# Fifteen products of the identity by itself on TensorE in the opening of a macaron block

## The chip, the cores and the metric

The kernel runs on one core of one Trainium2 chip. The metric is device time in microseconds (us) of one execution of the whole program; lower is better. The time before is the median of three runs. The profile is of one further execution.

## What is computed

The reference is a block of three residual steps over x, 2048 tokens of 1024 values in float32: half a feed-forward step, an attention step over a three-tap convolution, and the same feed-forward step again. The change touches the opening of the first feed-forward step, so that part is what must be seen:

```python
def _L0_ffn_ref(x, weight, bias, gate_w, in_channel_scale, out_channel_scale):
    ...
    router_logits = xf @ gate_w.T
    routing = jax.nn.softmax(router_logits.astype(jnp.float32), axis=1).astype(x.dtype)
    in_scale = routing @ in_channel_scale
    out_scale = routing @ out_channel_scale
    wb = ste_sign(weight)
    out = xf * in_scale @ wb.T * out_scale + bias
...
x = x + 0.5 * _L0_ffn_ref(_layernorm(x, axis=-1), L0_ffn_weight, ...)
x = x + _L0_attn_ref(_layernorm(x, axis=-1), ...)
x = x + 0.5 * _L0_ffn_ref(_layernorm(x, axis=-1), L0_ffn_weight, ...)
```

There are 8 experts, so the router's logits are 8 columns wide. The main product takes the sign of a 1024 x 1024 weight.

## The kernel before

The tokens are worked in 16 tiles of 128 rows. Each tile of a feed-forward step goes through the same stages, which are methods of the class `Ffn`:

- `norm_sums` takes mean and variance on VectorE (`bn_stats`, L164), the power on GpSimd (L171), and hands back a function that applies the normalization (on VectorE, L177, for the first tiles). The result is the tile `xn_f`.
- `transpose` (L216) turns `xn_f` on TensorE by products with the identity in transpose mode, eight of 128 x 128, four to a PSUM bank `tr_f`. ScalarE copies each bank to `xnT_f` (L217).
- `gate` (L224) multiplies by the gate's weights: eight products into four groups of 32 columns of `lgp_f`. ScalarE copies the result to `lgs` (L232).
- `route` (L237 to L249) adds the four groups by one product with `fold` (`lg_f`), takes the maximum on VectorE (L239), the exponential on ScalarE (`ro_f`, L242), and splits the routing into two parts (`rhl_f`).
- `turn` (L256) transposes the routing on TensorE (`rt_f`); VectorE copies it to `rT_f` (L258).
- `scale` (L268) makes the input scale of each channel by eight products `is_f` of `rT_f` with `tables`; VectorE multiplies (L279), ScalarE casts (`y_f`, L281), and the remainder is taken on VectorE or GpSimd (L282).
- `main` (L307) is the big product: for each of eight chunks, two halves of 512 columns and two parts of `y_f`, against `sw`, the signs of the weight. VectorE scales the sums and adds them to x (L319, L320).

The signs are made by ScalarE from the loaded weight rows (`sign`, L653, 1024 columns at a time). `tables` comes from two small tensors, worked on ScalarE (L136) and VectorE (L140, L146).

The opening is in the function `begin` (from L640). It is written in an order of its own: inside `tc.manual_schedule()` (L746) every instruction is issued on its engine in the order of the program text. `begin` issues the loads: the gate's rows on ScalarE's queue (L659), x and the weight on SyncE's queue (L660 to L669), the tables on GpSimd's queue (L130). Then it transposes the gate's rows (`gt`, L674, eight products with an output of 128 x 8 each), copies them to `gate_sb` (L675), and takes tiles 0 and 1 step by step through the stages up to the big product of tile 0 (L719), in which the stages of tiles 1 and 2 are placed between chunks (`beside`, L711). Behind `begin`, `ffn.run(2)` works the remaining tiles.

`ident` is the 128 x 128 identity in float32 that GpSimd makes at the very start (L106). PSUM tiles come from four pools of two banks each, "mm", "acc", "tr" and "sm", through the function `bank` (L73); a pool gives out its two buffers in turn. In the opening, "acc" is first used by `out_scale` (`po_f`, L291).

Of the kernel before, what the change touches and what calls it, by code (L numbers as in the profile page):

```python
# [17 lines left out]
P = 128  # L18
# [6 lines left out]
def kernel(  # L25
# [22 lines left out]
    nc = tc.nc  # L48
# [24 lines left out]
    def bank(kind, shape, name):  # L73
        return banks[kind].tile(shape, F32, name=name, tag=kind)
# [21 lines left out]
    def load_x(t):  # L96
        x1[t] = xring.tile([P, D], F32, name=f"x1_{t}", tag="x1")
        nc.sync.dma_start(out=x1[t], in_=x[ts(t, P), :])
# [6 lines left out]
    ident = const.tile([P, P], F32, name="ident")  # L105
# [12 lines left out]
    def small_constants():  # L118
        nc.vector.tensor_copy(fold, ident[:, 0:E])
        for j in range(1, 4):  # L120
            nc.vector.tensor_tensor(fold, fold, ident[:, ds(j * QC, E)], ALU.add)
        half = ident.rearrange("p (g h j) -> p g h j", g=4, h=2)[:, :, 1, :]
        nc.vector.tensor_reduce(lower, half, AX.XY, ALU.add)
        nc.vector.tensor_scalar(sides, lower, -2.0, 1.0, ALU.mult, ALU.add)

    def table_loads(raw):

        for n, src in enumerate((ics, ocs)):
            for h in range(NH2):
                nc.gpsimd.dma_start(  # L130
                    out=raw[ts(2 * n + h, QC), :],
                    in_=src[:, ts(h, NB)].unsqueeze(0).broadcast_to([4, E, NB]),
                )

    def upper_terms(raw, upper, n):
        nc.scalar.copy(upper[ts(n, P // 2), :], raw[ts(n, P // 2), :])  # L136

    def lower_terms(raw, n):
        at = ts(n, P // 2)
        nc.vector.tensor_scalar(raw[at, :], raw[at, :], lower[at, :], None, ALU.mult)  # L140

    def table_terms(raw, upper, n):


        at = ts(n, P // 2)
        nc.vector.scalar_tensor_tensor(  # L146
            tables[at, :], upper[at, :].bitcast(F32), sides[at, :], raw[at, :], ALU.mult, ALU.add
        )
# [35 lines left out]
    class Ffn:  # L184
# [13 lines left out]
        def norm(self, t, pinned=False, on_vector=False):  # L198
            for n in range(t, min(t + 2, self.end)):
                self.ahead(n)  # L200
            self.norm_sums(t, pinned, on_vector)()
# [207 lines left out]
    def x2_sums(t):  # L409
        xn = x2ns[t] = xnp.tile([P, D], F32, name=f"x2n_{t}", tag="xn")  # L410
        x2[t] = spill.tile([P, D], F32, name=f"x2_{t}")
        nc.sync.dma_start(out=x2[t], in_=x1[t])

        return sums_of(xn, x1.pop(t), f"x2_{t}", on_vector=2 * (t + 1 == NT))
# [225 lines left out]
    def begin(ffn, work):  # L640

        raws = {}

        def load_raw(c):
            pl, tag = (cwp, "cw") if c < 6 else (xring, "x1")
            raws[c] = pl.tile([P, D], F32, name=f"raw_{c}", tag=tag)
            nc.sync.dma_start(out=raws[c], in_=weight_t[ts(c, P), :])

        def sign(*chunks):
            for c in chunks:
                nc.scalar.activation(sw[:, c, :], raws[c], AF.Sign)  # L653


        rows = work.tile([P, D], F32, name="gate_rows", tag="osc")[0:DC, :]
        tmp = work.tile([P, D], F32, name="tables_raw", tag="osc")
        raw, upper = tmp[:, 0:NB], tmp[:, NB:D].bitcast(F32R)
        nc.scalar.dma_start(out=rows, in_=gate_t.rearrange("(c p) e -> c (p e)", p=P))  # L659
        load_x(0)  # L660
        load_x(1)
        for c in range(DC):
            load_raw(c)
            if c == 5:
                load_x(2)
        nc.sync.dma_start(out=hbias, in_=bias.broadcast_to([P, D]))
        load_x(3)
        load_x(4)
        load_x(5)  # L669
        table_loads(raw)  # L670
        small_constants()
        gt = bank("sm", [P, E, DC], "gt")
        for e in range(E):
            nc.tensor.transpose(gt[:, e, :], rows.rearrange("c (p e) -> c e p", e=E)[:, e, :], ident[0:DC, 0:DC])  # L674
        nc.scalar.copy(gate_sb[:, :, 0:E], gt.rearrange("p e c -> p c e"))  # L675
        on_vector = (nc.vector.tensor_copy,) * 2
        ffn.norm_sums(0, on_vector=2)()
        norm = ffn.norm_sums(1, on_vector=1)
        ffn.transpose(0)
        norm()  # L680
        ffn.gate(0)
        upper_terms(raw, upper, 0)
        ffn.route(0, lambda: lower_terms(raw, 0))
        table_terms(raw, upper, 0)
        ffn.transpose(1)
        ffn.turn(0)
        sign(0, 1)
        ffn.scale(0, lows=(nc.vector, nc.gpsimd))
        upper_terms(raw, upper, 1)
        lower_terms(raw, 1)  # L690
        table_terms(raw, upper, 1)
        ffn.gate(1)
        sign(2)
        norms = {}

        def part(*steps):
            def run():
                for stage, *a in steps:
                    stage(*a)
            return run  # L700

        def halve():
            nc.scalar.mul(hbias, hbias, 0.5)

        def sums(t, on_vector=False):
            norms[t] = ffn.norm_sums(t, on_vector=on_vector)

        def apply(t):
            norms.pop(t)()

        beside = {  # L711
            1: part((sign, 3), (ffn.route, 1), (sums, 2, 1)),
            2: part((sign, 4), (apply, 2)),
            3: part((ffn.turn, 1), (sign, 5)),
            4: part((sign, 6), (ffn.scale, 1), (sign, 7), (halve,), (ffn.add_bias, 1)),
            5: part((ffn.transpose, 2, on_vector), (sums, 3, 1)),
            6: part((ffn.out_scale, 0), (ffn.gate, 2)),
        }
        ffn.main(0, 0, 1, beside=beside, apart=DC - 2)  # L719
        ffn.add_bias(0)  # L720
        apply(3)
        ffn.out_scale(1)
        ffn.add_bias(2)
        rest = []
        ffn.main(1, 0, beside={
            2: part((ffn.route, 2), (sums, 4)),
            4: part((ffn.transpose, 3), (apply, 4), (ffn.add_bias, 4)),
            6: part((ffn.turn, 2)),
        })
        ffn.gate(3)  # L730
        ffn.scale(2, out=True)
        ffn.add_bias(3)
        ffn.main(1, 1, beside={
            3: part((ffn.route, 3), (ffn.transpose, 4)),
            5: part((ffn.turn, 3)),
            6: lambda: (rest.append(x2_sums(0)), sums(5)),
        })
        ffn.gate(4)
        rest[0]()
        apply(5)  # L740
        ffn.add_bias(5)

    with ExitStack() as ph:
        work = pool(ph, "work1", 2, side="right")
        ffn = Ffn("f1", sw, work, xnp, 0, NT, lambda t: x1[t], next_x, norm_x2, transpose_x2, beside)
        with tc.manual_schedule():  # L746
            begin(ffn, work)
        for dst, src in ((conv_b_sb, conv_b), (bq_sb, bq), (bk_sb, bk), (bv_sb, bv), (bo_sb, bo)):
            tc.keep_in_program_order(nc.sync.dma_start(out=dst, in_=src))
        ffn.run(2)  # L750
# [331 lines left out]
```

## Time and profile before

| what | value |
|---|---|
| median of three runs | 976.1 us (974.65 to 977.55) |
| profiled execution, its own time | 974.22 us |
| span of the profiled execution | 972.0 us |
| DMA, first slice of 24.3 us | 337 GB/s |
| DMA over the whole span | 141 GB/s |
| identity ready (end of its last step on GpSimd) | 1.54 us |
| end of the gate's transposes on TensorE | 4.15 us |
| start of the first transposes of tile 0 | 7.41 us |
| start of the first big product of tile 0 | 16.68 us |

The span runs from the first to the last instruction that the profile shows; the time of an execution has a little around it (974.22 against 972.0). Times inside the execution are counted from the span's start. A row of the timeline names the engine, the line of the kernel, the output and the inputs, their shapes, and in brackets how long the engine sat idle before it and who released it. The chain of waits is the sequence of work that ended last, followed back from the last instruction; each step is either an instruction or the gap between two ("issue"). Engines: PE is TensorE (PEld its loads of the stationary operand), DVE is VectorE, ACT is ScalarE, POOL is GpSimd, SP is SyncE.

### The profile page before, as it was taken

Reading aid. Unit: us, or ns where it says so; the run is one execution under the profiler, and the core shown is the slowest. Engines: PE = TensorE matmul, PEld = TensorE weight load, DVE = VectorE, ACT = ScalarE, POOL = GpSimd, SP = SyncE. Lnnn points to the kernel's source line nnn. Section 1 sums busy time; section 2 is a strip of 40 time slices with the busy share of each in tenths; the row PEclk is TensorE's granted clock in tenths of the full one; section 3 lists DMA queues with packets and bytes.
Section 4 is the critical chain, followed back from the end, with each engine's and each line's share of the span. In section 5 each row is a group of like instructions: output and inputs, shape, how many; then the busy total and the mean of one; then the engine's idle time right before and its main releaser. Section 6 shows DMA issues by size and latency. Waiting matters only on the chain.

```text
span 972.0 us, 13861 instructions
## 1 busy us (share of the span) xinstructions
PE 952.3 (98%) x5064; PEld 623.5 (64%) x5064; DVE 638.0 (66%) x1228; ACT 409.6 (42%) x1122; POOL 250.4 (26%) x319
## 2 busy tenths in 40 slices
PE   6999999999999999999999999999999999999997
PEld 4688778876666666645555455545554556878776
DVE  5788887799986566537656455646555655666654
ACT  5586665421111111126545344536451653444441
POOL 2555443410011101004213121212122312444341
PEclk9999999999999999999999999999999999999999
DMA  9776554698487665235020430044004216646331
GB/s 337 173 199 192 154 174 145 240 246 329 153 260 204 176 172 139 77 134 203 27 104 1 169 109 5 1 157 146 1 0 154 56 31 219 171 135 174 104 109 65
DMA packets 37522, 137.21 MB, mean 141 GB/s; under 512 B 4872, under 2 KB 5896, under 8 KB 35536
## 3 DMA queue, kind: packets, MB, share of 16 engines
q1 hardware_dynamic: 28336, 98.69, 27.9%
q0 software_dynamic: 8384, 29.63, 16.1%
q10 hardware_dynamic: 736, 8.02, 2.2%
q8 instruction: 40, 0.66, 0.3%
q14 instruction: 26, 0.21, 0.1%
HBM read 81.70 MB, written 37.85 MB: 123 GB/s over the span
## 4 chain that ended last, share of the span: by engine, by line
PE 60%; issue 27%; POOL 5%; DVE 3%; DMA 2%; ACT 2%; POOLq 0%; DVEq 0%; ACTq 0%
PE pm_f L307 22%; PE cv L540 22%; POOL xr L857 3%; PE tr_f L216 3%; PE pp L991 2%; PE lgp_f L224 2%; DMA x<-in_x_dram 2%; POOL p L913 2%; PE acc L972 2%; PE is_f L268 1%; PE tr L427 1%; PE pq L880 1%; PE ao L955 1%; PE pt L942 1%; DVE st_f L164 1%
## 5 line engine op out<-in xcount | busy, mean ns | idle before, releaser
L307 PE MATMUL pm_f<-sw,y_f 128*128 128x512 f32 x1024 | 261.5, 406 | 0.6 <-ACT y_f L281 0.4
L307 PEld LDWEIGHTS pm_f<-sw,y_f 128*128 128x128 f32 x1024 | 187.1, 190 | 43.9 <-ACT y_f L281 0.8
L540 PE MATMUL cv<-v,u 128*128 128x342 f32 x576 | 166.0, 450 | 0.0
L540 PEld LDWEIGHTS cv<-v,u 128*128 128x128 f32 x576 | 109.0, 189 | 56.9 <-issue 0.3
L913 POOL TENSOR_SCALAR_AFFINE_SELECT p<-p 128x512 f32<-128x512 f32 x64 | 39.8, 646 | 280.9 <-ACT p L911 280.9
L926 ACT ACTIVATE p<-p,anm 128x128 f32<-128x128 f32 x256 | 99.0, 388 | 16.7 <-DVE anm L923 16.7
L282 POOL TENSOR_TENSOR y_f<-xnT_f,y_f 128x512 fp32r<-128x512 f32 x63 | 79.8, 1282 | 64.8 <-ACT y_f L281 64.8
L319 DVE TENSOR_TENSOR pm_f<-pm_f,os_f 128x512 f32<-128x512 f32 x64 | 44.6, 697 | 70.9 <-PE pm_f L307 70.7
L557 ACT ACTIVATE m<-cv 128x342 f32<-128x342 f32 x42 | 19.2, 457 | 158.7 <-PE cv L540 148.5
L911 ACT COPY p<-sc 128x512 f32<-128x512 f32 x64 | 34.3, 588 | 111.5 <-PE sc L901 111.4
L923 DVE TENSOR_REDUCE anm<-p 128x4 f32<-128x512 f32 x64 | 40.9, 681 | 47.6 <-POOL p L913 47.6
L972 PE MATMUL acc<-oT,wo_sb 128*128 128x512 f32 x128 | 67.2, 616 | 0.4 <-DVE oT L964 0.4
L880 PE MATMUL pq<-qkv,wq_sb 128*128 128x512 f32 x128 | 61.0, 596 | 0.0
L880 PE MATMUL pq<-qkv,wk_sb 128*128 128x512 f32 x128 | 60.1, 592 | 0.0
L540 PE MATMUL cv<-v,g 128*128 128x342 f32 (+2 forms) x224 | 57.1, 415 | 0.9 <-DVE v L462 0.9
L991 PE MATMUL pp<-pw_sb,o2T 128*128 128x512 f32 x128 | 57.4, 599 | 0.4
L864 PE MATMUL pv<-wv_sb,qkv 128*128 128x512 f32 x128 | 56.1, 592 | 0.0
L217 ACT COPY xnT_f<-tr_f 128x512 f32<-128x512 f32 x62 | 35.9, 587 | 47.7 <-PE tr_f L216 47.7
L540 PEld LDWEIGHTS cv<-v,g 128*128 128x128 f32 x224 | 39.7, 190 | 17.6 <-DVE v L462 1.3
L528 DVE SCALAR_TENSOR_TENSOR u<-g,u 128x1024 f32<-128x1024 f32 x18 | 22.0, 1220 | 41.5 <-issue 23.5
L926 ACT ACTIVATION_READ_ACCUMULATOR p<-p,anm 128x1 f32 x256 | 47.8, 187 | 0.0
L934 DVE TENSOR_TENSOR p<-p,asum 128x512 f32<-128x512 f32 x64 | 45.6, 712 | 2.2
(138 smaller groups left out, 1462.7 us busy)
## 6 DMA issues: line engine op xcount, KB each, us to landing
g<-in_conv_w_dram SPq DMA_DIRECT2D x28, 512.0 KB, 4.9
u<-in_conv_w_dram POOLq DMA_DIRECT2D x24, 512.0 KB, 6.1
x<-in_x_dram SPq DMA_DIRECT2D x16, 512.0 KB, 4.6
raw<-in_weight_t_dram SPq DMA_DIRECT2D x16, 512.0 KB, 6.0
x<-hbias POOLq DMA_DIRECT2D x16, 512.0 KB, 5.5
x<-x SPq DMA_DIRECT2D x16, 512.0 KB, 4.3
xr<-x SPq DMA_DIRECT2D x16, 512.0 KB, 6.9
x<-xr SPq DMA_DIRECT2D x16, 512.0 KB, 3.2
```

The lines of the kernel that those rows point to most:

```text
L282: lows[h].tensor_tensor(yl, y, yh.bitcast(F32), ALU.subtract)
L307: ins = nc.tensor.matmul(pms[h], lhsT=y[:, n, c, :], rhs=self.sw[:, c, ts(h, NB)], start=(c == 0 and n == 0), stop=(c == DC - 1 and n == 1),)
L319: nc.vector.tensor_tensor(pms[h], pms[h], o, ALU.mult)
L540: nc.tensor.matmul(accs[w, k][:, lo:hi], lhsT=uk[:, c, :], rhs=V[k][:, c, lo:hi], start=(c == 0), stop=(c == DC - 1),)
L864: nc.tensor.matmul(pv, lhsT=qkvs[g][2][:, c, ts(b, P)], rhs=wv_sb[:, c, ts(half, NB)], start=(c == 0), stop=(c == WC - 1),)
L880: nc.tensor.matmul(pq, lhsT=w_sb[:, c, ts(hp, P)], rhs=qkvs[g][n][:, c, :], start=(c == 0), stop=(c == WC - 1),)
L913: nc.gpsimd.affine_select(out=p, in_=p, pattern=[[0, BPG], [-1, P]], compare_op=ALU.is_ge, fill=NEG_INF, base=0, channel_multiplier=1,)
L923: nc.vector.tensor_reduce(nmax, p, AX.X, ALU.max, negate=True)
L926: nc.scalar.activation(p[:, b, :], p[:, b, :], AF.Exp, bias=nmax[:, b : b + 1], accum_out=asum[:, b : b + 1],)
L934: nc.vector.tensor_tensor(p, p, asum.unsqueeze(2).broadcast_to([P, BPG, P]), ALU.mult)
L972: nc.tensor.matmul(accs[g][m], lhsT=wo_sb[:, hp, ts(m, P)], rhs=oT, start=(hp == 0), stop=(hp == NHP - 1),)
L991: nc.tensor.matmul(pp, lhsT=o2T[:, m, ts(b, P)], rhs=pw_sb[:, m, ts(h, NB)], start=(m == 0), stop=(m == WC - 1),)
```

## The change

A PSUM tile `idle` of 128 x 128 is taken from the pool "acc", and a function `keep_busy` multiplies the identity by itself into it, so many times. It is called in seven places of `begin`: three products ahead of the gate's transposes and six behind them, one between gate and routing of tile 0, one ahead of and two behind the turn of tile 0, and two behind the gate of tile 1. Nothing reads the tile `idle`. The order of the other instructions on TensorE, and everything on the other engines, stays as it is. The first of the products waits for GpSimd, which the gate's transposes did before.

```diff
         small_constants()
+        idle = bank("acc", [P, P], "idle")
+
+        def keep_busy(times):
+
+            for _ in range(times):
+                nc.tensor.matmul(idle, lhsT=ident, rhs=ident, start=True, stop=True)
+
+        keep_busy(3)
         gt = bank("sm", [P, E, DC], "gt")
         for e in range(E):
             nc.tensor.transpose(gt[:, e, :], rows.rearrange("c (p e) -> c e p", e=E)[:, e, :], ident[0:DC, 0:DC])
         nc.scalar.copy(gate_sb[:, :, 0:E], gt.rearrange("p e c -> p c e"))
+        keep_busy(6)
         on_vector = (nc.vector.tensor_copy,) * 2
         ffn.norm_sums(0, on_vector=2)()
         norm = ffn.norm_sums(1, on_vector=1)
         ffn.transpose(0)
         norm()
         ffn.gate(0)
+        keep_busy(1)
         upper_terms(raw, upper, 0)
         ffn.route(0, lambda: lower_terms(raw, 0))
         table_terms(raw, upper, 0)
         ffn.transpose(1)
+        keep_busy(1)
         ffn.turn(0)
+        keep_busy(2)
         sign(0, 1)
         ffn.scale(0, lows=(nc.vector, nc.gpsimd))
         upper_terms(raw, upper, 1)
         lower_terms(raw, 1)
         table_terms(raw, upper, 1)
         ffn.gate(1)
+        keep_busy(2)
         sign(2)
```

## The prediction

> **What bounds the kernel now.** I read the page from the top. TensorE is busy 98% of the span, so almost everywhere a microsecond moves the end only if it is TensorE's own. The exception is the opening, the first slice of the page.
>
> ```profile
> span 972.0 us, 13861 instructions
> PE 952.3 (98%) x5064; PEld 623.5 (64%) x5064; DVE 638.0 (66%) x1228; ACT 409.6 (42%) x1122; POOL 250.4 (26%) x319
> ...
> PE   6999999999999999999999999999999999999997
> ...
> PEclk9999999999999999999999999999999999999999
> ```
>
> See the single 6 at the left: TensorE is less than 70% busy in the first 24.3 us. The clock row reads full there; the next view, the TensorE timeline of the opening, says otherwise (start, length, operation, count):
>
> ```profile
> 3.13 1.02 PE L674 MATMUL gt<-ident,gate_rows 8*128 8x8 f32 x8 [3.13 <-DMA gate_rows<-in_gate_t_dram]
> 7.41 1.97 PE L216 MATMUL tr_f<-ident,xn_f 128*128 128x128 f32 x8 [3.26 <-DVE xn_f L177]
> ...
> 11.54 1.95 PE L216 MATMUL tr_f<-ident,xn_f 128*128 128x128 f32 x8
> ...
> 20.04 3.76 PE L307 MATMUL pm_f<-sw,y_f 128*128 128x512 f32 x8
> ...
> 25.98 0.67 PE L268 MATMUL is_f<-rT_f,tables 32*128 32x128 f32 x8 [0.26 <-DVE rT_f L258]
> ...
> 27.64 1.05 PE L216 MATMUL tr_f<-ident,xn_f 128*128 128x128 f32 x8
> ```
>
> The same eight transposes take 1.95 to 1.97 us up to 13.5 us and 1.05 us at 27.64. Taking off the last one's own length (median 0.27 us warm, up to 0.475 us cold), one follows another after 0.216 us early and 0.111 us late. The 512-column products between 20.6 and 25.1 us start 0.426 us apart; later sixteen take 3.83 us, 0.24 each. So TensorE runs at half speed until somewhere between 25.1 and 26.0 us, although the granted-clock row shows 1.00 all along. I read the clock from the spacing, not from that row.
>
> Last, the chain of waits of the opening, which says whose time counts:
>
> ```profile
> 7.41 1.98 PE tr_f L216 x8
> ...
> 10.05 0.69 PE lgp_f L224 x8
> ...
> 11.09 0.59 PE lg_f L237 x2
> 11.69 1.81 PE tr_f L216 x8
> 13.50 0.02 issue
> 13.52 0.59 ACT xnT_f L217
> 14.11 1.90 ACT sw L653 x2
> 16.01 0.00 issue
> 16.02 0.63 ACT y_f L281
> ...
> 25.73 0.21 DVE rT_f L258
> 25.94 0.04 issue
> 25.98 0.67 PE is_f L268 x6
> ```
>
> From 7.41 to 13.50 TensorE has 5.07 us of the chain. From 13.52 to 25.73 it has none: ScalarE and VectorE carry it (signs, casts, router and norm of the next tiles). From 25.98 on TensorE is the chain again. So the slow products from 16.7 to 25.7 cost nothing; only the slow work before 13.5 us can be won.
>
> **The change part by part.** Fifteen products are added on TensorE and nothing else: order and waits of the other four engines stay as they are. Their output takes one buffer of the two-buffer pool "acc", so the users after it swap their two banks; no wait is added, cost nothing.
>
> Price of one: the trace has no 128x128 f32 product with a full stationary operand, but it shows that an f32 product is issued as two matrix instructions (lg_f: one call, x2), and each is a 128-column pass like a transpose. So 2 x 0.216 = 0.43 us slow, 2 x 0.111 = 0.22 us fast. Ends: 0.43, and 0.50 if loads don't overlap (two loads of lg_f: 0.50 us). I take 0.43, the transpose being the nearer shape.
>
> - Three before the gate's transposes. The identity is ready at 1.54 us: 1.6 to 2.9 us, beside the wait for gate_rows (3.13). At 0.50 each they end at 3.1. Hidden; gate_sb is ready at 5.74 and first needed at 9.31.
> - Six behind them: from 4.15 us, 6 x 0.43 = 2.6, to 6.75 (7.15 at 0.50). The transposes of tile 0 wait for xn_f until 7.41. Hidden, with 0.3 to 0.7 us to spare.
> - One after the gate of tile 0: its waiter, lg_f, waits for ScalarE until 11.09; lgp_f ends at 10.74. Hidden.
> - One before and two after the turn (rt_f), two after the gate of tile 1: what they cost depends on the clock, below. The last two stand before products that are not on the chain; free.
>
> What they can win is the clock. **If TensorE is fast from 7.4 us**, I walk the chain again. Transposes of tile 0: the second half of xn_f comes at 7.81, so they end at 7.85 + 3 x 0.111 + 0.27 = 8.46 instead of 9.38; the two copies (0.59 each) end at 9.24 instead of 10.01. Second half of the gate 0.40 instead of 0.69, copy lgs 0.27: 9.97 instead of 11.04. lg_f 10.01 to 10.29 instead of 11.68. Here VectorE takes over: it normalizes tile 1 until 10.93, so the maximum starts at 10.95 instead of 11.72, and tile 1's transposes at 10.97 instead of 11.54. Their halves end at 11.58 and 12.02; the copies end at 12.79 instead of 14.11, **1.3 us earlier**. The other branch: ro_f 11.14, the routing halves until 12.3, table terms and rT until 13.25, is_f 0.67, product on VectorE done at 14.67; the signs (2.0 us of ScalarE) end at 14.7, the cast y_f follows at 14.70 to 14.79 instead of 16.02. I take 1.25 us. The raw weights must have landed for signs 1.3 us earlier: issued from 1.6 us on with 7.2 to 12.5 us to landing, the first two arrive about 9 to 11 us. After that the chain is free of TensorE until 25.98, so the 1.25 us arrives there whole, and TensorE-bound work carries it to the end. The identities then hide: rt_f waits for its input until 12.35 while the transposes' last issue is at 11.75; two of 0.22 after rt_f end before rT (13.25).
>
> **If it stays slow**, the transposes of tile 1 issue until 13.27, the identity pushes rt_f from 13.28 to 13.70, two more put is_f at 14.78 instead of 14.18. Its product on VectorE is then done at 16.58, where y_f could go at 16.02: **0.6 us lost**.
>
> **Does the clock turn in time?** Row first: it turned 5.1 to 5.9 us after the stream that began at 20.04, and not in 7.4 to 19 us, when TensorE was busy 1.5 to 2.0 us of each 2 but with gaps, transposes and quarter-array products. The added work with the gate's transposes runs from 1.6 to 6.75, 5.15 us: by the row the turn falls at 6.7 to 7.5 us, just at the first transposes. The Trainium skill, "TensorE: Matmul & The Clock Gate", Part 1, has a free-running window of about 3.4 us that must be filled; a stretch of 5.15 us holds a whole one in about half of the phases ((5.15 - 3.4)/3.4), more if a nearly full one does. A rule that speaks against the change, same page, Part 4: transpose mode does not count as busy and does not get the fast clock. The row contradicts the second half here (0.216 against 0.111 us). If it held, only lgp_f and lg_f would shrink: the copies would end 0.6 us earlier, not 1.3. The first half no run here shows; if true, the gate's transposes cut the stretch, 2.6 us alone fills no window, and the gain is lost.
>
> **The rivals.**
> 1. Fast from about 7 us: -1.25 us. For: the stretch is as long as the one that turned it. Chance 0.52. Kept fast afterwards: at 42 to 46 us TensorE is busy only 2.3 of 4 us, and remains fast.
> 2. Slow side: the gate's small transposes (8 columns each) don't count, no window fills, and the identities stand before rt_f and is_f in the way: +0.6. It decides if spacing at 11.5 us is still 0.216. Chance 0.25.
> 3. Turns late, between the two tiles' transposes: only tile 1's are fast. They still start at 11.69, copies end at 13.5: -0.6. Chance 0.23.
> 4. That the time does not follow the clock: DMA moves about 400 GB/s until 23 us; if a load of weights lands later than I place it, the signs stay and case 1 becomes -0.3 or so. Within 3's chance.
>
> **The numbers.** The profiled execution took 974.22 us with a span of 972.0; the three timed runs have a median of 976.1, 1.9 above. I apply the shift to the median: case 1 gives 974.9, case 2 976.7, case 3 975.5. The runs of before spread by 2.9 us, which is also the 0.3% that a measurement of this kernel can tell from no change; no case reaches it. The range holds the three cases and about 1.5 us of spread on each side: 973.2 to 977.8. Faster by over 0.3% needs case 1 with a low draw: 0.10. Slower: case 2 with a high one, 0.06. Within: 0.84.
>
> **What would show it.** In the trace of after: identities end before 7.1 us; transposes of tile 0 then tile 1 in about 1.1 us each; the sign after the copies at about 12.7 instead of 14.01; y_f at about 14.75; is_f of tile 1 at about 24.7 instead of 25.98; every later row earlier by the same. Wrong if spacing at 11.5 us is 0.216, if rt_f and is_f come late, if the signs wait for a DMA, or if the shift at 26 us is gone by 100 us, where the chain passes a load of x (92.38, 7.16 us).

## The result: slower by 0.2%, and the profile after

The changed kernel takes 977.50 us (median of 22 runs, 974.97 to 981.09) where the kernel before takes 975.72 us (22 runs, 974.12 to 977.55): a ratio of 1.0021, 95% interval 1.0013 to 1.0028. That is within the 0.3% called no change in the prediction, but it is a loss of 1.8 us, where a gain of 1.2 was forecast. The runs after are also spread more widely than those before, over 6.1 us instead of 3.4.

The profiled execution after took 977.07 us. First its page:

```profile
span 974.9 us, 13920 instructions
PE 955.2 (98%) x5094; PEld 626.5 (64%) x5094; DVE 638.0 (65%) x1228; ACT 409.2 (42%) x1122; POOL 250.1 (26%) x319
...
PE   7999999999999999999999999999999999999997
...
PEclk9899999999999999999999999999999999999999
```

The first slice is fuller, as it must be with 30 instructions added. New is the 8 in the clock row: in the second slice, from 24.4 to 48.7 us, the granted clock is below full. Before, that row had no dip. The timeline of TensorE in the opening (start, length, operation, count) shows the gain and the loss:

```profile
4.15 2.93 PE L677 MATMUL idle<-ident 128*128 128x128 f32 x12
7.49 1.11 PE L216 MATMUL tr_f<-ident,xn_f 128*128 128x128 f32 x8 [0.41 <-DVE xn_f L177]
...
11.16 1.06 PE L216 MATMUL tr_f<-ident,xn_f 128*128 128x128 f32 x8 [0.65 <-DVE nm_f L239]
...
18.50 2.08 PE L307 MATMUL pm_f<-sw,y_f 128*128 128x512 f32 x8
...
24.65 1.11 PE L268 MATMUL is_f<-rT_f,tables 32*128 32x128 f32 x8 [1.99 <-DVE rT_f L258]
...
27.56 1.91 PE L216 MATMUL tr_f<-ident,xn_f 128*128 128x128 f32 x8
...
34.90 1.20 PE L307 MATMUL pm_f<-sw,y_f 128*128 128x512 f32 x4 [0.23 <-DVE x L320]
```

Up to 24.65 us everything goes nearly as in the first case of the prediction. The transposes of both tiles take 1.1 us instead of 1.95, and the scale of tile 1 (`is_f`) starts at 24.65 instead of 25.98, 1.33 us early. But the eight big products at 18.50 now take 2.08 us instead of 3.76, so TensorE runs ahead of ScalarE and VectorE and waits: 1.99 us stand in the bracket at 24.65. Then the same `is_f` takes 1.11 us instead of 0.67 and the transposes of tile 2 take 1.91 instead of 1.05. TensorE is slow again, now where it is the chain. The chain of waits after (start, length, step) says what that costs:

```profile
24.39 0.21 DVE rT_f L258
24.61 0.04 issue
24.65 1.11 PE is_f L268 x6
25.76 2.00 PE pm_f L307 x4
27.76 1.71 PE tr_f L216 x8
29.47 1.71 PE pm_f L307 x4
```

From `is_f` to the first big product of tile 1 takes 10.25 us (24.65 to 34.90) where it took 7.36 before (25.98 to 33.34): 2.89 us lost on a gain of 1.33, so 1.56 us late. Where the clock changed, and after what, is seen in stretches of 3.41 us (stretch, its length, busy time and count of PE, PEld, DVE, ACT and POOL, granted clock, DMA share, GB/s):

```profile
17.40:20.81 3.41, 2.32 (x10) 1.63 (x10) 2.13 (x5) 3.36 (x7) 1.22 (x1) 1.00 1.03 408
20.81:24.23 3.42, 1.22 (x5) 0.74 (x5) 2.65 (x7) 2.51 (x3) 0.55 (x1) 1.00 0.98 365
24.23:27.64 3.41, 2.99 (x13) 2.38 (x14) 1.65 (x4) 1.12 (x2) 0.42 (x1) 0.50 0.52 160
27.64:31.05 3.41, 3.41 (x13) 2.62 (x11) 2.23 (x4) 2.00 (x3) 3.10 (x3) 0.50 0.39 118
31.05:34.47 3.42, 3.42 (x29) 2.17 (x28) 1.72 (x5) 1.24 (x3) 0.56 (x1) 1.00 0.90 189
```

Behind the stretch in which TensorE worked only 1.22 us of 3.42, the clock goes to 0.50; two stretches later it is back. The stretches were chosen so because the trace's clock records lie on this grid: a rise at 7.16, a fall at 24.23 (five times 3.41 later), a rise at 31.05 (twice 3.41). The record of before rises at 26.03 us, so that execution, too, began slow; the clock row reads 1.00 ahead of the first record of an execution although the products run at half speed there.

### The profile page after: what moved, and what is told of

The parts are those of the page before. It is cut to its first block, busy times and chain, and to the rows that moved or that the text cites. A ratio compares the mean times of both kernels' runs of the same rounds, so it can differ in the third digit from the quotient of the medians.

```text
span 974.9 us, 13920 instructions
## 1 busy us (share of the span) xinstructions
PE 955.2 (98%) x5094; PEld 626.5 (64%) x5094; DVE 638.0 (65%) x1228; ACT 409.2 (42%) x1122; POOL 250.1 (26%) x319
## 4 chain that ended last, share of the span: by engine, by line
PE 57%; issue 28%; POOL 6%; DVE 4%; DMA 3%; ACT 2%; POOLq 0%; DVEq 0%; ACTq 0%
PE cv L540 22%; PE pm_f L307 20%; POOL xr L870 3%; PE tr_f L216 3%; PE pp L1004 2%; DMA x<-in_x_dram 2%; PE lgp_f L224 2%; POOL p L926 2%; PE acc L985 2%; PE is_f L268 1%; PE pq L893 1%; PE tr L427 1%; PE ao L968 1%; DVE st_f L164 1%; PE pt L955 1%
```

## The experiments

**Theory A:** the early rise is real and worth 1.3 us, but it makes TensorE run out of work at 16 to 24 us, and the clock falls just before TensorE becomes the chain. **Rival B:** the added products, or the two swapped accumulator banks, cost time by themselves. **Rival C:** it is the six later products, four of them in front of `lg_f`, `rt_f` and `is_f` of tile 0, that are in the way.

The opening is compared at one row, the first big product of tile 1 (33.34 us before, 34.90 after). Clock changes are those of the trace's records, in us, without the fall that closes each execution; the ratio is to the kernel before, timed in the same round.

| kernel | that row | clock | median, us | ratio (95% interval) |
|---|---|---|---|---|
| e1_fill | 32.05 | up 7.32 | 975.06 | 0.9997 (0.9989 to 1.0005) |
| e5_last_gap | 34.39 | up 16.23 | 976.93 | 1.0016 (1.0007 to 1.0025) |
| e2_nine | 32.15 | up 7.84, down 18.08, up 24.90 | 975.27 | 0.9999 (0.9990 to 1.0007) |
| e3_six | 35.91 | up 11.72, down 25.37, up 32.20 | 977.71 | 1.0024 (1.0016 to 1.0031) |
| e4_three | 33.33 | up 24.12 | 975.63 | 1.0000 (0.9992 to 1.0008) |
| e6_ten | 31.93 | up 7.42, down 17.66, up 24.49 | 976.08 | 1.0007 (1.0000 to 1.0014) |
| e7_nine_two | 32.83 | up 9.96, down 13.37, up 23.61 | 977.87 | 1.0020 (1.0012 to 1.0028) |
| e8_ten_fill | 33.22 | up 10.33, down 13.75, up 20.57 | 976.97 | 1.0013 (1.0006 to 1.0020) |
| e9_front_fill | 31.98 | up 5.98 | 975.12 | 0.9998 (0.9990 to 1.0006) |
| e10_front | 32.41 | up 6.67, down 13.50, up 23.74, down 102.24, up 109.07 | 975.43 | 1.0004 (0.9995 to 1.0014) |
| a1_again | 37.12 | up 16.06, down 26.30, up 33.13 | 980.61, one run | |
| a2_again | 34.02 | up 9.25, down 19.49, up 22.91, down 26.32, up 29.73 | 976.80, one run | |

### Filling the later holes: e1_fill and e5_last_gap

```diff
-            1: part((sign, 3), (ffn.route, 1), (sums, 2, 1)),
+            1: part((keep_busy, 4), (sign, 3), (ffn.route, 1), (sums, 2, 1)),
...
-            3: part((ffn.turn, 1), (sign, 5)),
-            4: part((sign, 6), (ffn.scale, 1), (sign, 7), (halve,), (ffn.add_bias, 1)),
+            3: part((keep_busy, 3), (ffn.turn, 1), (sign, 5)),
+            4: part((keep_busy, 7), (sign, 6), (ffn.scale, 1), (sign, 7), (halve,), (ffn.add_bias, 1)),
```

> The changed kernel plus 14 more identity products in TensorE's three later holes: four ahead of the routing of tile 1, three ahead of its turn, seven ahead of its scale. Theory A (the clock falls at 24.2 us because TensorE has too little to do from 16 to 24 us): the clock stays at 1.00 through 24 to 31 us, the eight is_f of tile 1 take about 0.67 us instead of 1.11 and the transposes of tile 2 1.05 instead of 1.91, the first big product of tile 1 starts at about 32.0 us (before 33.34, after 34.90), and the median falls to about 974.5, 3 us under the changed kernel. Rival B (the added products or the swapped accumulator banks cost time by themselves): 14 more products make it slower than the changed kernel, 978 or more, whatever the clock does.

The TensorE timeline of e1_fill:

```profile
16.96 1.05 PE L677 MATMUL idle<-ident 128*128 128x128 f32 x8
...
20.55 0.83 PE L677 MATMUL idle<-ident 128*128 128x128 f32 x6
...
22.58 1.73 PE L677 MATMUL idle<-ident 128*128 128x128 f32 x14
24.73 0.66 PE L268 MATMUL is_f<-rT_f,tables 32*128 32x128 f32 x8 [0.42 <-DVE rT_f L258]
...
26.36 1.06 PE L216 MATMUL tr_f<-ident,xn_f 128*128 128x128 f32 x8
...
32.05 1.20 PE L307 MATMUL pm_f<-sw,y_f 128*128 128x512 f32 x4 [0.24 <-DVE x L320]
```

and two of its stretches:

```profile
17.56:20.97 3.41, 3.09 (x19) 2.52 (x18) 2.22 (x5) 3.36 (x7) 1.14 (x1) 1.00 1.01 401
20.97:24.39 3.42, 3.21 (x23) 2.67 (x21) 2.65 (x7) 2.43 (x3) 0.55 (x1) 1.00 0.93 335
```

With 14 more products the opening is 2.85 us faster than the changed kernel's (32.05 against 34.90). Rival B has no room for that. The stretch ahead of 24.4 us has 3.21 us of work instead of 1.22, the clock stays up, and `is_f` and the transposes keep their 0.66 and 1.06 us. The median is 2.4 us below the changed kernel's, but only 0.4 below before, less than its interval. The 974.5 expected took an early rise for every run; how many had one is not known.

e5_last_gap fills only the third hole:

> The changed kernel plus seven identity products in the last hole alone (22.7 to 24.6 us, ahead of the scale of tile 1). Theory A: the window of 3.41 us that ends at 24.2 us then has about 2.9 us of work instead of 1.4 and the clock stays up: like the kernel with all three holes filled, first big product of tile 1 at about 32.0 us, median about 974.5. If an earlier hole (16.3 to 18.3 us) also matters, the clock falls at about 20.8 us and the gain is partly lost. Rival B: same as the changed kernel or slower, 977.5 to 978.5.

The profile is inconclusive for its question: in that execution the clock did not rise until 16.23 us, and stayed up. It shows something else: with the clock low in the first tile, the identities stand in the way, and the row is 1.05 us late without any fall. The timed runs add to this, by their mean clocks (how they are read is said under "What remains open"): only four of 14 have a fall behind the start, but the median of the other ten is 977.3 us. So keeping the clock from falling is not enough; what made these ten slow is shown for the profiled one alone, by its late rise.

### The nine alone and the six alone: e2_nine and e3_six

```diff
         keep_busy(3)
...
         keep_busy(6)
...
-        keep_busy(1)
...
-        keep_busy(1)
         ffn.turn(0)
-        keep_busy(2)
...
-        keep_busy(2)
```

> Only the nine products around the gate's transposes, without the six in the waits. Theory A: the clock still rises at about 7.2 us, and with even less work afterwards falls by 24.2 us at the latest: first big product of tile 1 at 34 to 35 us, median 976.5 to 978, no better than before. Rival C (the six are what costs, because they stand in front of rt_f and is_f): then this one gains what was forecast, first big product of tile 1 at about 32.1 us, median about 974.5.

Wrong for theory A as it was put. TensorE's timeline and stretches of e2_nine:

```profile
18.39 0.60 PE L237 MATMUL lg_f<-fold,lgs_f 128*128 128x8 f32 x2 [1.21 <-ACT lgs_f L232]
18.84 3.76 PE L307 MATMUL pm_f<-sw,y_f 128*128 128x512 f32 x8
...
24.78 0.70 PE L268 MATMUL is_f<-rT_f,tables 32*128 32x128 f32 x8 [0.26 <-DVE rT_f L258]
...
32.15 1.19 PE L307 MATMUL pm_f<-sw,y_f 128*128 128x512 f32 x4 [0.25 <-DVE x L320]
```

```profile
14.66:18.08 3.42, 1.47 (x5) 0.67 (x4) 1.41 (x3) 2.02 (x5) 0.59 (x1) 1.00 1.03 412
18.08:21.49 3.41, 3.10 (x8) 2.58 (x9) 2.65 (x7) 3.39 (x7) 0.68 (x1) 0.50 1.02 404
21.49:24.90 3.41, 3.15 (x10) 1.88 (x8) 2.51 (x6) 1.97 (x3) 0.55 (x1) 0.50 0.91 298
```

The clock falls here too, but at 18.08 us, where TensorE is ahead anyway. At half speed the big products fill the wait that would have been idle, the clock is up again at 24.90, behind the second of those stretches, and `is_f` at 24.78 is early by 1.20 us and nearly all fast. So theory A needs a second half (A'): a fall is harmless at 18 us and costly at 24 us, and the six decide which. They add work to the stretch around 14 to 17 us (2.63 us in the changed kernel, 1.47 here), so that the fall comes later. The six alone:

```diff
-        keep_busy(3)
         gt = bank("sm", [P, E, DC], "gt")
...
-        keep_busy(6)
```

> Only the six products in the waits of tiles 0 and 1, without the nine around the gate's transposes. Theory A: the clock is low at 7 us and, with TensorE at work from 7.4 us on, rises somewhere before 26 us. If it rises only at 24 to 26 us: rt_f and is_f of tile 0 come 0.4 and 0.6 us late, first big product of tile 1 at about 33.9 us (before 33.34), median about 976.3. If it rises at 17 or 21 us, it can fall again and cost like the changed kernel (34.9 us). Rival C (the six cost by themselves): 977.5, with the loss already there at 24 us.

The profile shows neither time of rise that was expected. The clock rose at 11.72 us, in time for tile 1's transposes and too late for tile 0's; `rt_f` and `is_f` of tile 0 were 0.16 and 0.12 us late, not 0.4 and 0.6. Then the clock fell at 25.37 us, behind a stretch with 1.23 us of work, and the row is 2.57 us late. Just before that, `is_f` of tile 1 started at 25.65, still 0.33 us early. So the loss is not there at 24 us, and it is not the six's own length: rival C falls in this form. The median, 977.71, is like the changed kernel's.

### What is not the clock: e4_three

```diff
         keep_busy(3)
...
-        keep_busy(6)
...
-        keep_busy(1)
```

and so on: only the first three are left, so the bank swap and the added tile stay.

> Only the first three products, ahead of the gate's transposes, so the swapped accumulator banks and the added tile stay but the clock has no reason to rise early. Theory A: 1.3 us of products fill no window; clock and opening as before, first big product of tile 1 at 33.2 to 33.5 us, median 975.5, ratio to before 1.000. Rival B (bank swap or added products cost by themselves): 0.5 us or more slower.

As expected: the row is at 33.33 against 33.34 and the ratio is 1.0000, so the added tile and the swapped banks cost nothing. The clock rose at 24.12, almost 2 us earlier than in the profile of before, and the row moved by only 0.01 us: what TensorE does slowly between 24 and 26 us is indeed off the chain.

### One product more, two of the six, and the fill without them: e6_ten, e7_nine_two, e8_ten_fill

These are e2_nine with `keep_busy(7)` for `keep_busy(6)`; e2_nine with the `keep_busy(2)` behind `ffn.gate(1)`; and e6_ten with the three fills of e1_fill.

> Three ahead of the gate's transposes and seven behind them, none in the later waits: the kernel with nine, with the stretch longer by 0.43 us. Theory A' (the six hold the clock up too long; without them it falls at 17 to 18 us, where TensorE is not on the chain, and is up again by 25 us): first big product of tile 1 at about 32.1 us when the clock rose at 7 us; a longer stretch holds a whole window of 3.41 us more often, so median a little under the nine's: 974.5 to 975.2. Seven end at 7.1 to 7.2 us, before the transposes of tile 0 at 7.4 to 7.7. If the phase of the window plays no part, the time of all runs lies together at 974.3.

The opening is as expected, 1.41 us early. The median is not: 976.08, from 974.44 to 980.05. In the profiled execution 0.9 of the 1.4 us is gone at 100 us, where the chain passes a load of x. Why the median of this one is worse than the nine's stays open.

> The nine and, of the six, only the two ahead of the first big product of tile 0. Theory A': these two (0.45 us at 14.5 to 15.2 us) lie in the window that lets the clock fall at 17 to 18 us in the kernel with nine. If they are enough to hold it there, it falls one or two windows later (21 to 24.5 us) and costs like the changed kernel: first big product of tile 1 at 34 to 35 us, median 977. If they are not enough, it is as with nine: 32.1 us and 975.3. Rival C (it is the place before rt_f and is_f that costs): as with nine, whatever the clock.

The profiled execution took another course (up at 9.96, down at 13.37) and answers nothing. The median is 977.87, 2.6 us over the nine's, with two products that stand in front of neither `rt_f` nor `is_f`. That fits A' and not rival C, but no trace shows this kernel with a fall at 21 to 24.5 us.

> Ten around the gate's transposes, none in the waits of tile 0, and the three later holes filled (4, 3 and 7). Theory A: with an early rise the clock either stays up to the end or falls by 18 us and the fill brings it back before 25: first big product of tile 1 at 32.0 to 32.3 us. With a late rise the 14 stand in TensorE's way at half speed (14 x 0.43 = 6 us in holes of about 4 us when fast): up to 2 us lost. Median 974.5 to 976, more spread than with ten alone.

The clock rose at 10.33 and fell at 13.75; the four fills at 18.7 us then took 1.91 us and `is_f` of tile 1 started at 25.90, where the changed kernel's started at 24.65. The row is 33.22, outside what was expected for an early rise. The median is 0.13% above before: the fill that helps in e1_fill does not help here. That the early fall is the reason is shown for the profiled execution only.

### The changed kernel again: a1_again and a2_again

> The changed kernel once more, for another draw of the phase of the 3.41 us window (counted from the start, the clock's changes lay 0.33 us after a multiple of 3.41 in its first profile). Theory A: which row is slow follows from the phase. If the clock rises at 7 to 8 us it falls again between 20 and 25 us and the first big product of tile 1 starts 1 to 2 us late (34.3 to 35.5); if it rises at 10 to 12 us, tile 0 is slow in part, and it falls between 20 and 26 us; if it rises after 15 us, is_f of tile 0 is 0.6 to 1 us late and that stays.

> As the run before: the changed kernel, a further draw of the phase. Rival B (a fixed cost of the added products): the same 34.9 us whatever the clock did.

The same program, three profiles, and the row at 34.90, 37.12 and 34.02 us: 1.56, 3.78 and 0.68 us late, 2.0 us on average, where the medians differ by 1.8. A fixed cost (rival B) would give one number. Why a1_again did not rise at 7 us is in its first stretches:

```profile
2.41:5.83 3.42, 3.42 (x20) 3.17 (x20) 1.42 (x4) 1.50 (x2) 1.75 (x4) 1.00 0.95 344
5.83:9.24 3.41, 2.78 (x13) 2.48 (x13) 2.58 (x7) 0.38 (x1) 0.86 (x4) 1.00 1.04 325
```

The first is busy from end to end and does not lift the clock: the gate's eight small transposes lie in it (3.2 to 4.2 us), and busy in the profile's sense is not what counts. The same holds for the like stretches of a2_again, e5_last_gap, e7_nine_two and e8_ten_fill, each busy for 3.41 us with 0.7 to 1.0 us of these transposes in it. The timeline of a1_again shows the rest:

```profile
7.71 1.97 PE L216 MATMUL tr_f<-ident,xn_f 128*128 128x128 f32 x8 [0.63 <-DVE xn_f L177]
...
15.21 1.05 PE L268 MATMUL is_f<-rT_f,tables 32*128 32x128 f32 x8
...
26.98 1.11 PE L268 MATMUL is_f<-rT_f,tables 32*128 32x128 f32 x8 [1.98 <-DVE rT_f L258]
...
37.12 1.19 PE L307 MATMUL pm_f<-sw,y_f 128*128 128x512 f32 x4 [0.23 <-DVE x L320]
```

`is_f` of tile 0 is 1.0 us late (14.18 before): `xn_f` came 0.3 us later, and the slow identities in front of it make up the other 0.7. Then the clock falls at 26.30 all the same: both losses in one execution.

### A version meant to win: e9_front_fill, and e10_front

```diff
-        keep_busy(3)
+        early = const.tile([P, 1], F32, name="early")
+        nc.scalar.copy(early, nhalf)
+        keep_busy(11)
         gt = bank("sm", [P, E, DC], "gt")
...
-        keep_busy(6)
```

e9_front_fill has this on top of e1_fill, e10_front on top of e2_nine.

> Eleven products in one stretch from 1.6 to 6.3 us, the gate's transposes behind them, a small copy at the start so that ScalarE's table is loaded before; the six in the waits and the three filled holes as in e1_fill. Theory A: the stretch of 4.7 us holds a nearly full window (2.9 us of 3.41) in about two phases of three, where 2.9 us plus the transposes do in about one of three; the fill then keeps the clock up. Opening 1.3 us earlier in those: first big product of tile 1 at about 32.0 us; median 974.4 to 975.0, ratio to before 0.999. If the clock rises late, up to 1 us lost. Rival B: with 28 products the slowest of all.

In stretches, the start of e9_front_fill, to be read against the first line of a1_again above (the same place on the grid, and as busy):

```profile
2.57:5.98 3.41, 3.41 (x18) 3.41 (x17) 1.59 (x5) 0.24 (x2) 1.60 (x3) 1.00 0.95 353
```

With the gate's transposes moved out of it, this stretch lifts the clock, at 5.98 us (as the first full one of e10_front does, at 6.67), and the row is at 31.98, 1.36 us early. The median is 0.45 us under before, ratio 0.9998, not told apart from no change. It does beat the changed kernel, by 2.4 us, as e1_fill does; neither is shown to beat the kernel before.

> The same stretch of eleven, none of the six and no fill. Theory A: an earlier rise (5 to 8 us) makes the fall come at 15 to 21 us, and the clock is up again two or three windows later: where it fell by 18 us, no loss (first big product of tile 1 at 32.1 us); where it fell at 20 to 22 us, up to 1.5 us lost at 25 to 29 us. Median between 974.5 and 976.5, wider spread than before.

The row is 0.93 us early, with a fall already at 13.50. Then a second fall, at 102.24 us: TensorE waited 1.85 us for a load of x, and two slow stretches followed. At 107 us this execution is 3.6 us behind the profile of before. So the opening is not the only place where a wait can bring a fall.

## Why the prediction was wrong

**What held.** The reading that the opening of before runs at half speed until about 26 us (its record rises at 26.03), and that the slow work behind 13.5 us costs nothing: e4_three moves the rise by 2 us and the row by 0.01, and e2_nine, slow from 18.08 to 24.90 us, is still 1.19 us early. The price of a product: the six behind the gate's transposes take 2.93 us at half speed, the seven of e6_ten 3.35, so 0.42 us for one where 0.43 was forecast. The walk of the chain: `is_f` of tile 1 1.33 us early for 1.25.

**The step that failed** is "so the 1.25 us arrives there whole", with its ground "Kept fast afterwards: at 42 to 46 us TensorE is busy only 2.3 of 4 us, and remains fast". The prediction walked the chain with fast TensorE times but did not lay out TensorE's own timeline with them. The work from 16 to 25 us is done in about half the time, while the deadline stays with ScalarE and VectorE; what is left are waits, and the stretch ahead of 24.23 us has 1.22 us of work, well under the ground (2.3 of 4 us there, or 1.73 of 3.41 in the stretch that begins at 43.10). So the term "slow again after 24 us" was put at nothing; it is worth 2.89 us in the profiled execution, more than twice the gain that was summed.

**The gate's transposes** were the doubt of rival 2, and rightly: stretches filled by them in part did not lift the clock, stretches as full without them did (a1_again against e9_front_fill). But the Trainium skill's rule that transpose mode does not count as busy ("TensorE: Matmul & The Clock Gate", Part 4) does not hold for the 128-column transposes of the tiles. In e7_nine_two the clock rises at 9.96 us behind this stretch:

```profile
6.54:9.96 3.42, 3.06 (x19) 2.02 (x18) 2.56 (x6) 1.10 (x2) 0.96 (x5) 1.00 1.07 323
```

2.0 us of its work are such transposes, 0.5 us identities and 0.6 us products of the gate; e8_ten_fill rises at 10.33 us behind the same mix. How much is needed is close: in a2_again 1.2 us of identities and 1.6 us of transposes, 2.87 us in all, lifted the clock at 9.25 us, and the same mix with 2.78 us did not in a1_again and e5_last_gap. The page's window of about 3.4 us in Part 1 agrees with every record of this case.

**The chances.** An early rise was given 0.52, and no case had a fall behind it. In the three profiles of the changed kernel the clock rose at 7.16, 16.06 and 9.25 us, and fell again each time. Rival 2's price of 0.6 was near: `is_f` of tile 0 was 1.0 us late in a1_again, 0.3 of it because `xn_f` came later (7.71 for 7.41). But rival 2 ended there, and the execution lost 2.8 us more by the fall. That the measured median lies inside the range is luck: no case gave more than 0.6 us of loss, and the range left only 1.1 us above that case, not the 1.5 named.

**What remains open.** After the opening the profiles part further, by 0.2 to 4.5 us, at the loads of x (80 to 150 us) and in the attention step (500 to 700 us). At least part of this is not a matter of the change: e4_three, whose opening equals that of before, ends 1.43 us later than the profile of before, whose 974.22 us is a low draw of that kernel. The timed runs give one mean clock each, and it tells whether the clock fell, though not where. The fall at the very end takes at most 2.7 us of the span in the fourteen profiles, which leaves a mean of 0.9986; a mean of 0.997 or less needs a fall further in. Of the changed kernel's 22 runs 20 have one, of e3_six's 15 thirteen, of e1_fill's 13 and e4_three's 13 none, of 129 of the kernel before nineteen. So the fall is the rule in the changed kernel and not an accident of its profiles. It is no loss by itself: nine of e2_nine's 13 runs have one, with a median of 974.47 us against 975.93 for the other four. When the clock rose is not in that mean, so how the 1.8 us divide between falls near 24 us and late rises stays open.

## What to carry to other kernels

Speeding up an engine while it is not the chain makes it wait, and on TensorE such a wait had a price that fell later: ask what it will be doing in the last 3.4 us before it becomes the chain again, and redraw its own timeline, not only the chain's. Padding that lifts the clock has to hold it until the work is dense, as in e1_fill, or let it drop early enough to be back by then, as in e2_nine; dropped just before the dense work it cost more than a clock first lifted at 26 us (34.90 against 33.34). Compare the position of one row over several profiles: where the place of a grid decides that differs from one execution to the next, one profile is one draw.

## What the runs showed of the hardware

- In these traces the clock changes only on a grid of 3.41 us, whose place differs from execution to execution: what remains of the first rise after whole steps of 3.41 us lies anywhere between 0.1 and 3.3 us.
- In the opening, falls came behind stretches with 1.22 to 2.08 us of profiled work in 3.41 (after 1.22, a1_again 1.29, e2_nine 1.47, e7_nine_two 2.08), and not behind 2.20 (e2_nine) or 2.32 (after); but the kernel before stays up at 43.10 to 46.51 us with 1.73. So the profile's busy time is not the measure itself.
- A stretch that is busy throughout did not lift the clock in five executions in which 0.7 to 1.0 us of it were products of 8 rows by 8 columns, nor in e10_front from 102.24 to 105.66 us, where 2.0 us were products that use 32 rows or 32 columns.
- The clock row reads 1.00 until the first change of an execution. Only the spacing of equal instructions (0.216 against 0.111 us in the kernel before) shows the slow start.
